# New places in the written-out order of a Mamba and FP4 feed-forward kernel on one core

## The chip, the core and the metric

The kernel runs on one core of a Trainium2 chip. Its engines are TensorE (PE in the profile, with its weight loads shown apart as PEld), VectorE (DVE), ScalarE (ACT), GpSimd (POOL) and SyncE (SP), which here issues all DMAs. The metric is the time of one launch in microseconds (us) on the device. Three runs of the kernel before gave a median of 1878.63 us (1877.05 to 1879.68).

## The reference, cut to what matters

The input x has 8 sequences of 2048 tokens with 256 features. A state-space layer and a feed-forward layer follow each other, each with a residual and a layer norm behind it. In the feed-forward layer the activations and the weights are rounded to a grid of FP4 values with one scale per 16 features.

```python
def _L0_attn_ref(x, W_in, conv_w, conv_b, W_xproj, A_log, D, W_out):
    x_proj, z = jnp.split(x @ W_in, 2, axis=-1)          # 512 channels each
    xc = conv(x_proj, 4 taps along the tokens, one filter per channel)
    x_conv = silu(xc + conv_b)
    ssm = x_conv @ W_xproj                               # 1 + 16 + 16 columns
    delta = softplus(ssm[..., 0])
    Bm, Cm = ssm[..., 1:17], ssm[..., 17:]
    h_mean = einsum('bld,bln->bdn', x_conv, delta[..., None] * Bm) / L
    y = einsum('bdn,bln->bld', h_mean, Cm) + D * x_conv
    return (y * silu(z)) @ W_out

def _L0_ffn_ref(x, w_gate, w_up, w_down):                # 704 hidden features
    h = silu(fp4_linear(x, w_gate)) * fp4_linear(x, w_up)
    return fp4_linear(h, w_down)                         # rounds x, h and the weights

x = layernorm(x + _L0_attn_ref(x, ...))
x = layernorm(x + _L0_ffn_ref(x, ...))
```

(The body of the convolution is shown in words.) h_mean is a mean over all tokens of a sequence: no token of a sequence can be finished before all of its tokens have been through the convolution.

## The kernel before

A **block** is 512 tokens of one sequence, so there are 32 blocks, four to a sequence. A **pair** is 256 tokens, half a block; its two pairs are called even and odd here (half 0 and half 1). Blocks and pairs are numbered from 0.

`begin_block` takes one block as far as the sums over tokens, channels on the partitions: `load` (SP), and for each of four groups of 128 channels `project` (PE, L601), `halo` (POOL), `fetch` (ACT), `first` (ACT, the first tap), three `tap` (DVE, L621), `silu` (ACT, L627), and later `skip` (ACT, the product with D). Then, for the whole block, `x_projection` (PE, L634), `keep_ssm` (ACT) and `by_token` (DVE). For each of four chunks of 128 tokens: `turn` (PE, L663, transposes into one PSUM buffer), `turned` (ACT, L669, copies that buffer to SBUF) and `weigh` (DVE, L674, reads the same buffer and makes delta's input). The softplus is small DVE work on 128x4 elements: `negate` (L501), `exp` (POOL, L504), `ratio` (L508 to L514), `series`, `delta`, then `delta_b` (L653, writes dB). `sums` (PE, L688) adds the block to its sequence's state, and behind a sequence's last block `mean`, `spread_mean` (L702) and `keep_mean` (L708) make hT.

`mix_block` works four blocks later (LAG): `state` (PE, L750, four PSUM buffers) and four `mix` (DVE, L761).

`finish_pair` does the rest for a pair: `zed` (PE, L794), `silu_z` (ACT), `gated` (POOL, L810, a product of two SBUF tiles), `out` (PE, L817), `residual1` (DVE, L827), layer norm 1 (`n1_stats` DVE, `n1_rstd` POOL, `n1_apply` ACT), and the rounding to FP4 (`q1_scales` L287 to L298, `q1_normalize` L310, `q1_magnify` ACT L318, `q1_add` L322, `q1_subtract` L326). Rounded values and scales then go to the other layout by DMA: `q1_turn_scales` (DVE), `q1_gather_scales` (four small DMAs to HBM), `q1_spread_scales` (one broadcast DMA back, tile q_s), `q1_turn` (a DMA transpose, tile q_gT); `q1_scale` (POOL, L391) multiplies the two. Gate and up run in three column groups (`gate`, `up` PE L840, `silu_g` ACT, `product` DVE L865). The hidden features go through the same rounding (`q2_...`, the broadcast now 704 KB, the product hqT of 128x1408), then `down` (PE, L871), `residual2` (DVE, L880), layer norm 2 and `store` (SP). The last pair goes through `finish_last` in two tiles of 128 tokens, which transposes on PE in place of DMAs.

The FP4 weights are made at the start, one rounding of gate, up and down each (`PREPARE`), between the first blocks' work.

Nothing decides the order at run time. Each piece of work is put into a list with a number, its *place*; a piece of block n has n times PERIOD added, and a finishing piece (n + LAG) times PERIOD. The list is sorted by place and the pieces are written out in this order, each instruction at the end of its engine's queue. So places say who stands behind whom in a queue; they are no times, and a unit of place is no microsecond. Buffers rotate in pools of fixed size (seven PSUM buffers of one bank in the pool `ps`), and the framework adds semaphore waits for data and for buffers.

```python
def at(base, table, name, index, f, *args):
    place = table[name]
    for i in index:
        place = place[i]
    events.append((base + place, len(events), f, args))
...
for _, _, f, args in sorted(events, key=lambda e: e[:2]):
    f(*args)
```

The places stand in four tables at the top of the file: BLOCK, PAIR (even, odd), LAST (the last pair's two tiles) and PREPARE (the weights).

Of the kernel before, what the change touches and what calls it, by code (L numbers as in the profile page):

```python
# [26 lines left out]
PERIOD = 64.0  # L27
LAG = 4
BLOCK = {
    "load": -56.2,  # L30
    "halo": (-37.7, -4.0, 38.9, 5.1),
    "project": (-2.4, 20.8, 60.7, 37.8),
    "fetch": (0.4, 26.0, 64.3, 42.7),
    "first": (15.9, 38.4, 64.5, 46.8),
    "tap": ((32.5, 53.3, 53.3), (66.1, 68.5, 74.6), (75.7, 77.2, 79.3), (67.1, 69.8, 78.4)),
    "silu": (75.3, 79.4, 88.1, 83.0),
    "skip": (190.0, 117.2, 116.7, 116.8),
    "x_projection": 97.8,
    "keep_ssm": 100.8,
    "by_token": 113.7,  # L40
    "negate": 116.9,
    "exp": 117.4,
    "ratio": 117.5,
    "series": (119.2, 119.3),
    "delta": 125.0,
    "delta_b": 126.2,
    "turn": (95.0, 93.9, 89.9, 99.5),
    "turned": (101.5, 107.0, 100.5, 115.5),
    "sums": 126.3,
    "mean": 128.4,  # L50
    "spread_mean": 133.4,
    "keep_mean": 134.7,
    "state": 77.4,
    "mix": (78.9, 77.5, 80.1, 77.9),
    "weigh": (104.6, 102.6, 97.0, 116.0),
}
# [42 lines left out]
LAST = {
    "out": (100.3, 121.0),  # L100
    "residual1": (137.9, 122.5),
    "n1_stats": (185.7, 133.0),
    "n1_rstd": (193.6, 133.1),
    "n1_apply": ((206.5,), (142.8,)),
    "q1_scales": (228.2, 169.0),
    "q1_normalize": (240.8, 172.9),
    "q1_magnify": (283.6, 192.6),
    "q1_add": (314.2, 201.7),
    "q1_subtract": (438.8, 201.9),
    "q1_scale": (452.3, 213.0),  # L110
    "turn_xq": (522.5, 215.8),
    "turned_xq": (543.6, 216.6),
    "gate_up": ((573.2, 587.2, 579.3), (326.7, 409.7, 380.2)),
    "silu_g": ((596.4, 631.2, 696.9), (403.3, 526.5, 405.8)),
    "product": ((617.5, 737.8, 704.0), (501.1, 551.9, 514.4)),
    "q2_scales": (776.2, 563.7),
    "q2_normalize": (842.6, 566.6),
    "q2_magnify": (861.1, 609.1),
    "q2_add": (963.3, 672.1),
    "q2_subtract": (993.0, 690.6),  # L120
    "q2_scale": (996.9, 705.7),
    "turn_h": ((1071.2, 1083.9), (827.7, 902.7)),
    "turned_h": ((1176.6, 1176.7), (882.6, 1019.9)),
    "down": (1214.9, 1030.2),
    "residual2": (1234.8, 1072.4),
    "n2_stats": (1280.2, 1143.6),
    "n2_rstd": (1324.6, 1241.6),
    "n2_apply": ((1395.9,), (1265.4,)),
    "store": (1488.6, 1392.9),
}  # L130
PREPARE = {
    "weights": 9.1,
    "load": (-47.3, 119.5, 195.3, 284.7, 342.4),
    "scales": (-4.4, 134.9, 205.0, 285.8, 345.2),
    "normalize": (13.6, 134.9, 221.0, 286.8, 345.3),
    "magnify": (15.9, 138.6, 222.0, 289.7, 353.8),
    "add": (83.1, 154.4, 228.8, 290.3, 358.3),
    "subtract": (96.7, 158.2, 229.8, 296.4, 360.2),
    "scale": (100.3, 170.3, 233.9, 301.2, 360.3),
    "turn": ((111.7,), (188.0, 186.6, 182.2), (252.6, 250.6, 273.0), (323.1, 329.9, 320.9, 326.8), (380.3, 387.2, 384.9, 373.7)),  # L140
}

@with_exitstack
# [973 lines left out]
```

## Time and profile before

| what | us |
|---|---|
| median of three runs (lowest to highest) | 1878.63 (1877.05 to 1879.68) |
| the profiled execution | 1877.57 |
| its span, first to last instruction | 1875.4 |
| mean clock granted to PE, share of full speed | 0.987 |

The profile is of one execution. A window's line gives, for a stretch of the span, its length, the busy time of each engine with the number of its instructions, the clock granted to PE as a share, the mean share of the DMA engines and the GB/s. A line of waits names who waited, for whom, the total in us, how often, and the longest. A line of a source line gives the number of its instructions, their least, median and greatest duration in ns, and the start of the first and the last. The clock of the first stretches of the page's slices is below one:

```profile
PEclk8899999999999999999999999999999999999997
```

Some rows of the costliest groups, for the size of the pieces (columns: busy us, mean ns of one, then idle time before):

```profile
L621 DVE SCALAR_TENSOR_TENSOR xc<-xp,cw_sb,xc 128x512 f32<-128x512 f32 x384 | 283.7, 752 | 4.9 <-ACT xc L615 3.6
...
L674 DVE SCALAR_TENSOR_TENSOR xd<-ps,w_delta_sb 128x512 bf16<-128x512 f32 x128 | 86.9, 679 | 77.0 <-ACT xct L669 76.0
```

### The profile page before, as it was taken

To read this page: it belongs to the slowest core of one execution; us is meant where nothing else is said; L and a number is where in the kernel's file an instruction comes from. 1 tells how busy PE (TensorE), PEld (TensorE's weight loads), DVE (VectorE), ACT (ScalarE), POOL (GpSimd) and SP (SyncE) were. 2 spreads that over 40 slices of the span, in tenths; PEclk is the share of its full clock that TensorE was granted. 3 is DMA by queue.
4 is the path that set the end of the run, shared out by engine and by line. 5 is a ranking of instruction groups with operands and counts; after the bars stand their busy time and mean duration, and the time that the engine had idled before them with its cause. 6 is when DMAs were issued, how large, how long until landed. Compare 5 with 4: busy or idle time off the path is not lost.

```text
span 1875.4 us, 28706 instructions
## 1 busy us (share of the span) xinstructions
PE 1815.0 (97%) x10062; PEld 1463.1 (78%) x10062; DVE 1669.2 (89%) x3087; ACT 836.1 (45%) x1426; POOL 906.5 (48%) x962
## 2 busy tenths in 40 slices
PE   5799999999999999999999999999999999999986
PEld 2468887888888888888888888788888888788874
DVE  6889999999999999899999999999999999877874
ACT  5664454444444444454444445444444444333222
POOL 1234554545454534554544554544545453465652
PEclk8899999999999999999999999999999999999997
DMA  3223344343344343434333334334334423454440
GB/s 103 67 62 85 86 100 104 82 102 92 83 104 100 83 98 90 96 93 100 93 91 98 91 85 101 103 82 102 92 80 105 103 75 84 85 114 103 100 87 23
DMA packets 248384, 170.11 MB, mean 91 GB/s; under 512 B 171952, under 2 KB 223024, under 8 KB 248240
## 3 DMA queue, kind: packets, MB, share of 16 engines
q1 hardware_dynamic: 248240, 168.28, 37.5%
q8 instruction: 80, 1.31, 0.3%
q14 instruction: 64, 0.52, 0.1%
HBM read 116.34 MB, written 20.91 MB: 73 GB/s over the span
## 4 chain that ended last, share of the span: by engine, by line
PE 72%; DVE 12%; POOL 7%; issue 5%; DMA 2%; ACT 2%; SPq 0%; POOLq 0%; DVEq 0%; ACTq 0%
PE ps L840 25%; PE ps L871 13%; PE ps L601 9%; PE ps L794 9%; PE ps L817 9%; PE ps L663 2%; DVE xc L621 2%; POOL ln_rs L552 2%; PE ps L750 1%; DVE q_amax L287 1%; PE hsum L688 1%; PE ps L634 1%; DVE q_x L310 1%; POOL ln_ve L550 1%; DMA q_s<-q_rows 1%
## 5 line engine op out<-in xcount | busy, mean ns | idle before, releaser
L871 PE MATMUL ps<-wdT,hqT 128*128 128x256 f32 x1512 | 343.6, 384 | 13.1 <-POOL hqT L391 12.9
L871 PEld LDWEIGHTS ps<-wdT,hqT 128*128 128x128 f32 x1512 | 287.5, 192 | 69.5 <-issue 17.4
L810 POOL TENSOR_TENSOR xc<-xc,sz 128x512 f32<-128x512 f32 x128 | 201.7, 1587 | 272.0 <-DVE xc L761 272.0
L840 PE MATMUL ps<-wuT,xqT 128*128 128x256 f32 (+1 forms) x1512 | 328.2, 363 | 2.1 <-DVE x L880 2.1
L840 PE MATMUL ps<-wgT,xqT 128*128 128x256 f32 (+1 forms) x1512 | 325.4, 364 | 0.3 <-POOL xqT L391 0.3
L840 PEld LDWEIGHTS ps<-wgT,xqT 128*128 128x128 f32 x1512 | 274.4, 191 | 64.3 <-issue 37.8
L840 PEld LDWEIGHTS ps<-wuT,xqT 128*128 128x128 f32 x1512 | 273.4, 190 | 43.2 <-issue 6.2
L621 DVE SCALAR_TENSOR_TENSOR xc<-xp,cw_sb,xc 128x512 f32<-128x512 f32 x384 | 283.7, 752 | 4.9 <-ACT xc L615 3.6
L550 POOL TENSOR_SCALAR ln_ve<-ln_mv 128x2 f32<-128x2 f32 (+1 forms) x130 | 75.7, 582 | 397.6 <-DVE ln_mv L545 390.9
L601 PE MATMUL ps<-xT,w_in_sb 128*128 128x512 f32 x512 | 243.4, 601 | 6.0 <-DMA xT<-in_x_t_dram 6.0
L318 ACT ACTIVATE q_w<-q_x 128x512 bf16<-128x512 f32 (+3 forms) x131 | 130.9, 999 | 256.6 <-DVE q_x L310 255.0
L794 PE MATMUL ps<-xTz,w_in_sb 128*128 128x256 f32 x1024 | 241.9, 379 | 0.0
L558 ACT ACTIVATE x<-x,ln_nb,ln_rs 128x256 f32<-128x256 f32 x256 | 142.8, 593 | 195.6 <-POOL ln_nb L555 178.3
L817 PE MATMUL ps<-w_out_sb,xc 128*128 128x256 f32 x1008 | 228.0, 379 | 0.0
L794 PEld LDWEIGHTS ps<-xTz,w_in_sb 128*128 128x128 f32 x1024 | 192.7, 190 | 25.0 <-issue 1.7
L817 PEld LDWEIGHTS ps<-w_out_sb,xc 128*128 128x128 f32 x1008 | 189.2, 190 | 24.7 <-POOL xc L810 0.2
L391 POOL TENSOR_TENSOR hqT<-q_gT,q_s 128x1408 f32<-128x1408 bf16 x63 | 181.2, 2877 | 2.4 <-DMA q_gT<-q_w 1.6
L858 ACT ACTIVATE sg<-ps 128x512 f32<-128x512 f32 (+1 forms) x189 | 104.8, 556 | 164.2 <-PE ps L840 115.8
L322 DVE SCALAR_TENSOR_TENSOR q_x<-q_w,q_x 128x512 f32<-128x512 bf16 (+3 forms) x131 | 159.3, 1216 | 4.0 <-ACT q_w L318 3.7
L601 PEld LDWEIGHTS ps<-xT,w_in_sb 128*128 128x128 f32 x512 | 95.8, 193 | 81.2 <-issue 76.1
L674 DVE SCALAR_TENSOR_TENSOR xd<-ps,w_delta_sb 128x512 bf16<-128x512 f32 x128 | 86.9, 679 | 77.0 <-ACT xct L669 76.0
L326 DVE SCALAR_TENSOR_TENSOR q_w<-q_w,q_x 128x512 bf16<-128x512 bf16 (+3 forms) x131 | 151.8, 1159 | 2.6
(115 smaller groups left out, 2487.3 us busy)
## 6 DMA issues: line engine op xcount, KB each, us to landing
q_s<-q_rows SPq DMA_DIRECT2D x63, 704.0 KB
xT<-in_x_t_dram SPq DMA_DIRECT2D x32, 512.0 KB
xTz<-in_x_t_dram SPq DMA_DIRECT2D x64, 256.0 KB
xt<-in_L_attn_x_dram SPq DMA_DIRECT2D x64, 256.0 KB
q_s<-q_rows SPq DMA_DIRECT2D x63, 256.0 KB
out_dram<-x SPq DMA_DIRECT2D x63, 256.0 KB
q_rows<-q_scT SPq DMA_DIRECT2D x252, 4.0 KB
q_rows<-q_scT SPq DMA_DIRECT2D x252, 12.0 KB
```

Of the source, the lines that this page charges most:

```text
L318: nc.scalar.activation(state["g"], state["x"], AF.Abs, scale=GRID)
L322: nc.vector.scalar_tensor_tensor(xn, w, 1.5 * GRID, xn, ALU.max, ALU.subtract)
L326: nc.vector.scalar_tensor_tensor(w, w, 1.5 * GRID, xn, ALU.max, ALU.subtract)
L391: nc.gpsimd.tensor_tensor(qT(), state["gT"], state["scT"], ALU.mult)
L558: nc.scalar.activation(r()[:, t, :], r()[:, t, :], AF.Identity, bias=v["nb"][:, t : t + 1], scale=v["rstd"][:, t : t + 1],)
L601: nc.tensor.matmul(mm, w_in_sb[:, k, c * P : (c + 1) * P], s["xT"][:, k, :], start=(k == 0), stop=(k == KM - 1),)
L621: nc.vector.scalar_tensor_tensor(acc, xp[:, k + 1 : k + 1 + T], cw_sb[:, c, k + 1 : k + 2], acc, ALU.mult, ALU.add)
L794: nc.tensor.matmul(q["mm", j][:, a, :], w_in_sb[:, k, DI + c * P : DI + (c + 1) * P], q["xT"][:, k, :], start=(k == 0), stop=(k == KM - 1),)
L810: nc.gpsimd.tensor_tensor(xc, xc, q["sz"][:, c, :], ALU.mult)
L817: nc.tensor.matmul(mm[:, t, :], s["xc"][:, c, o : o + P], w_out_sb[:, c, :], start=(c == 0), stop=(c == NC - 1),)
L840: nc.tensor.matmul(q[name, j][:, t, :n], q["xqT"][:, t * KM + k, :], wT[:, k, f0 : f0 + n], start=(k == 0), stop=(k == KM - 1),)
L871: nc.tensor.matmul(mm[:, t, :], q["hqT"][:, t * NF + j, :], wdT[t][:, j, :], start=(j == 0), stop=(j == NF),)
```

## The change

The numbers in the four tables are replaced by new ones; PERIOD, LAG, and everything below the tables stay. So every piece keeps its instructions, tiles and buffers and gets a new place in the order. The diff has a line for each name of the four tables; these are the ones that matter most for the text below.

```diff
 BLOCK = {
-    "tap": ((32.5, 53.3, 53.3), (66.1, 68.5, 74.6), (75.7, 77.2, 79.3), (67.1, 69.8, 78.4)),
-    "silu": (75.3, 79.4, 88.1, 83.0),
+    "tap": ((29.14, 47.51, 49.35), (61.51, 63.86, 69.02), (69.77, 71.43, 78.60), (70.57, 79.32, 81.67)),
+    "silu": (67.08, 83.05, 82.80, 86.47),
...
-    "x_projection": 97.8,
-    "keep_ssm": 100.8,
-    "by_token": 113.7,
-    "negate": 116.9,
-    "exp": 117.4,
-    "ratio": 117.5,
-    "series": (119.2, 119.3),
-    "delta": 125.0,
-    "delta_b": 126.2,
-    "turn": (95.0, 93.9, 89.9, 99.5),
-    "turned": (101.5, 107.0, 100.5, 115.5),
-    "sums": 126.3,
+    "x_projection": 100.62,
+    "keep_ssm": 103.94,
+    "by_token": 107.26,
+    "negate": 107.08,
+    "exp": 110.53,
+    "ratio": 114.55,
+    "series": (120.42, 120.73),
+    "delta": 123.06,
+    "delta_b": 123.24,
+    "turn": (100.18, 94.70, 93.30, 96.56),
+    "turned": (107.90, 101.13, 96.16, 120.33),
+    "sums": 128.44,
...
-    "weigh": (104.6, 102.6, 97.0, 116.0),
+    "weigh": (105.96, 103.03, 93.70, 106.97),
 }
 PAIR = {
...
-    "zed": ((24.7, 20.7), (56.5, 50.5)),
-    "silu_z": ((31.0, 31.3), (59.6, 62.5)),
-    "gated": ((81.4, 83.2), (94.3, 92.7)),
+    "zed": ((25.73, 31.85), (62.07, 64.54)),
+    "silu_z": ((31.50, 68.65), (70.65, 71.37)),
+    "gated": ((88.05, 89.53), (101.88, 108.23)),
...
-    "n1_rstd": (103.4, 130.9),
+    "n1_rstd": (104.18, 135.37),
...
-    "q1_normalize": (112.0, 139.2),
+    "q1_normalize": (114.24, 145.41),
...
-    "q1_add": (115.4, 151.8),
-    "q1_subtract": (115.9, 152.2),
+    "q1_add": (114.70, 155.11),
+    "q1_subtract": (115.32, 155.23),
...
-    "q1_spread_scales": (129.1, 153.4),
-    "q1_turn": (124.0, 156.4),
-    "q1_scale": (129.8, 158.1),
+    "q1_spread_scales": (124.94, 166.78),
+    "q1_turn": (126.58, 155.50),
+    "q1_scale": (129.41, 167.59),
...
-    "q2_scales": (156.3, 183.1),
-    "q2_normalize": (161.7, 188.6),
+    "q2_scales": (161.93, 183.91),
+    "q2_normalize": (163.51, 190.42),
...
-    "q2_add": (167.3, 197.3),
-    "q2_subtract": (168.8, 198.1),
+    "q2_add": (169.88, 203.89),
+    "q2_subtract": (175.66, 205.47),
...
-    "q2_turn": (177.9, 216.8),
-    "q2_scale": (185.5, 219.0),
-    "down": (189.0, 227.3),
-    "residual2": (205.2, 234.8),
-    "n2_stats": (213.2, 237.1),
+    "q2_turn": (181.09, 214.66),
+    "q2_scale": (182.53, 227.13),
+    "down": (192.05, 229.56),
+    "residual2": (199.43, 235.62),
+    "n2_stats": (214.13, 235.75),
...
-    "store": (221.3, 252.8),
+    "store": (223.66, 252.24),
...
 }
```

In BLOCK, `turn`, `turned` and `weigh` list the chunks 0 to 3, `silu` the channel groups; in PAIR the first number or group is the even pair's, the second the odd pair's. A piece at place 167 of one block and one at place 103 of the next stand side by side, since PERIOD is 64.

More of the change, by code (lines that the diff above doesn't have):

```diff
@@ L29 @@
 BLOCK = {
[L30 to L34, printed above, removed]
-    "tap": ((32.5, 53.3, 53.3), (66.1, 68.5, 74.6), (75.7, 77.2, 79.3), (67.1, 69.8, 78.4)),
-    "silu": (75.3, 79.4, 88.1, 83.0),
-    "skip": (190.0, 117.2, 116.7, 116.8),
-    "x_projection": 97.8,
-    "keep_ssm": 100.8,
-    "by_token": 113.7,
-    "negate": 116.9,
-    "exp": 117.4,
-    "ratio": 117.5,
@@ L44 @@
-    "series": (119.2, 119.3),
-    "delta": 125.0,
-    "delta_b": 126.2,
-    "turn": (95.0, 93.9, 89.9, 99.5),
-    "turned": (101.5, 107.0, 100.5, 115.5),
-    "sums": 126.3,
[L50 to L54, printed above, removed]
-    "weigh": (104.6, 102.6, 97.0, 116.0),
+    "load": -54.29,
+    "halo": (-6.72, -28.05, 58.44, 39.71),
+    "project": (-2.38, 26.50, 55.03, 38.59),
+    "fetch": (-2.03, 32.97, 60.17, 47.48),
@@ new lines @@
+    "first": (14.26, 40.15, 61.81, 52.44),
+    "tap": ((29.14, 47.51, 49.35), (61.51, 63.86, 69.02), (69.77, 71.43, 78.60), (70.57, 79.32, 81.67)),
+    "silu": (67.08, 83.05, 82.80, 86.47),
+    "skip": (210.79, 104.19, 208.26, 120.63),
+    "x_projection": 100.62,
[8 more added lines that the diff above has]
+    "turn": (100.18, 94.70, 93.30, 96.56),
@@ L56 @@
+    "turned": (107.90, 101.13, 96.16, 120.33),
+    "sums": 128.44,
+    "mean": 130.09,
+    "spread_mean": 130.55,
+    "keep_mean": 133.85,
+    "state": 73.25,
+    "mix": (80.53, 79.69, 79.90, 82.73),
+    "weigh": (105.96, 103.03, 93.70, 106.97),
 }
 PAIR = {
-    "load_t": (-19.1, 38.0),
-    "load_x": (90.8, 71.7),
-    "zed": ((24.7, 20.7), (56.5, 50.5)),
-    "silu_z": ((31.0, 31.3), (59.6, 62.5)),
-    "gated": ((81.4, 83.2), (94.3, 92.7)),
-    "out": (92.7, 123.2),
-    "residual1": (98.2, 127.2),
@@ L65 @@
-    "n1_stats": (101.2, 130.5),
-    "n1_rstd": (103.4, 130.9),
-    "n1_apply": ((105.3, 105.7), (133.1, 131.4)),
-    "q1_scales": (107.6, 134.8),
-    "q1_normalize": (112.0, 139.2),
-    "q1_magnify": (112.7, 141.2),
-    "q1_add": (115.4, 151.8),
-    "q1_subtract": (115.9, 152.2),
-    "q1_turn_scales": (110.5, 137.6),
-    "q1_spread_scales": (129.1, 153.4),
-    "q1_turn": (124.0, 156.4),
-    "q1_scale": (129.8, 158.1),
-    "gate": ((131.5, 133.6, 147.7), (171.1, 171.5, 167.3)),
-    "silu_g": ((134.9, 135.4, 150.8), (180.8, 177.5, 174.1)),
@@ L79 @@
-    "up": ((141.7, 144.2, 152.0), (178.5, 182.1, 167.6)),
-    "product": ((145.9, 150.8, 154.8), (181.7, 183.0, 177.0)),
-    "q2_scales": (156.3, 183.1),
-    "q2_normalize": (161.7, 188.6),
-    "q2_magnify": (164.9, 192.2),
-    "q2_add": (167.3, 197.3),
-    "q2_subtract": (168.8, 198.1),
-    "q2_turn_scales": (158.1, 185.0),
-    "q2_spread_scales": (170.8, 206.4),
-    "q2_turn": (177.9, 216.8),
-    "q2_scale": (185.5, 219.0),
-    "down": (189.0, 227.3),
-    "residual2": (205.2, 234.8),
@@ L92 @@
-    "n2_stats": (213.2, 237.1),
-    "n2_rstd": (216.2, 240.0),
-    "n2_apply": ((219.3, 220.8), (247.4, 243.4)),
-    "store": (221.3, 252.8),
-    "q1_gather_scales": (120.6, 152.1),
-    "q2_gather_scales": (163.1, 195.8),
+    "load_t": (-40.08, 58.48),
+    "load_x": (47.72, 66.29),
+    "zed": ((25.73, 31.85), (62.07, 64.54)),
+    "silu_z": ((31.50, 68.65), (70.65, 71.37)),
+    "gated": ((88.05, 89.53), (101.88, 108.23)),
+    "out": (95.70, 125.60),
+    "residual1": (99.36, 127.22),
@@ new lines @@
+    "n1_stats": (100.40, 130.53),
+    "n1_rstd": (104.18, 135.37),
+    "n1_apply": ((106.40, 106.98), (139.63, 139.26)),
+    "q1_scales": (110.08, 143.35),
+    "q1_normalize": (114.24, 145.41),
+    "q1_magnify": (114.33, 154.32),
+    "q1_add": (114.70, 155.11),
+    "q1_subtract": (115.32, 155.23),
+    "q1_turn_scales": (112.14, 152.30),
+    "q1_spread_scales": (124.94, 166.78),
+    "q1_turn": (126.58, 155.50),
+    "q1_scale": (129.41, 167.59),
+    "gate": ((139.28, 132.09, 148.78), (175.11, 173.33, 169.64)),
@@ new lines @@
+    "silu_g": ((142.54, 141.04, 149.47), (179.58, 174.55, 171.04)),
+    "up": ((151.87, 134.37, 148.79), (176.58, 174.21, 172.04)),
+    "product": ((152.91, 147.26, 150.59), (183.14, 183.10, 176.89)),
+    "q2_scales": (161.93, 183.91),
+    "q2_normalize": (163.51, 190.42),
+    "q2_magnify": (166.30, 194.41),
+    "q2_add": (169.88, 203.89),
+    "q2_subtract": (175.66, 205.47),
+    "q2_turn_scales": (163.17, 194.44),
+    "q2_spread_scales": (177.48, 211.11),
+    "q2_turn": (181.09, 214.66),
@@ L98 @@
+    "q2_scale": (182.53, 227.13),
+    "down": (192.05, 229.56),
+    "residual2": (199.43, 235.62),
+    "n2_stats": (214.13, 235.75),
+    "n2_rstd": (218.21, 245.24),
+    "n2_apply": ((222.77, 220.44), (249.66, 248.56)),
+    "store": (223.66, 252.24),
+    "q1_gather_scales": (123.69, 152.49),
+    "q2_gather_scales": (172.81, 208.53),
 }
 LAST = {
[L100 to L129, printed above, removed]
+    "out": (116.96, 124.39),
+    "residual1": (139.70, 137.78),
@@ new lines @@
+    "n1_stats": (144.79, 145.59),
+    "n1_rstd": (179.50, 151.75),
+    "n1_apply": ((184.83,), (160.37,)),
+    "q1_scales": (222.18, 167.58),
+    "q1_normalize": (249.49, 168.25),
+    "q1_magnify": (296.90, 178.65),
+    "q1_add": (348.21, 181.18),
+    "q1_subtract": (377.02, 197.36),
+    "q1_scale": (459.18, 209.24),
+    "turn_xq": (482.10, 211.41),
+    "turned_xq": (533.22, 214.19),
+    "gate_up": ((570.55, 571.33, 646.11), (305.18, 429.40, 437.31)),
+    "silu_g": ((579.04, 703.18, 708.77), (397.66, 459.08, 446.13)),
@@ new lines @@
+    "product": ((628.72, 757.14, 722.33), (397.78, 475.22, 479.00)),
+    "q2_scales": (790.70, 524.15),
+    "q2_normalize": (840.93, 536.49),
+    "q2_magnify": (870.91, 564.08),
+    "q2_add": (909.52, 581.47),
+    "q2_subtract": (949.66, 588.51),
+    "q2_scale": (1049.29, 612.74),
+    "turn_h": ((1110.93, 1050.67), (811.95, 792.95)),
+    "turned_h": ((1115.18, 1159.95), (813.51, 959.75)),
+    "down": (1207.39, 976.22),
+    "residual2": (1223.66, 1062.85),
+    "n2_stats": (1239.26, 1091.98),
@@ L130 @@
+    "n2_rstd": (1348.85, 1185.82),
+    "n2_apply": ((1418.49,), (1260.80,)),
+    "store": (1558.46, 1344.44),
 }
 PREPARE = {
[L132 to L139, printed above, removed]
@@ L140 @@
-    "turn": ((111.7,), (188.0, 186.6, 182.2), (252.6, 250.6, 273.0), (323.1, 329.9, 320.9, 326.8), (380.3, 387.2, 384.9, 373.7)),
+    "weights": 11.23,
+    "load": (-39.51, 112.43, 197.71, 273.33, 339.69),
+    "scales": (-33.38, 126.51, 210.44, 279.11, 339.70),
+    "normalize": (-17.33, 127.93, 215.67, 281.81, 340.59),
+    "magnify": (16.93, 130.87, 217.22, 286.26, 346.74),
+    "add": (53.14, 140.83, 222.52, 289.74, 354.07),
+    "subtract": (82.62, 153.80, 222.57, 290.03, 360.31),
+    "scale": (98.84, 159.37, 233.74, 296.53, 360.51),
@@ L141 @@
+    "turn": ((99.60,), (191.68, 187.04, 177.59), (272.17, 264.32, 253.93), (314.43, 315.67, 318.81, 328.50), (370.36, 382.98, 385.89, 363.76)),
 }
```

## The prediction

> **What bounds the kernel now.** I read the page's busy line first, then the windows of the stages, then the waits of TensorE (PE) and VectorE (DVE) in each stage, and last the rows of the instructions that the change moves past one another.
>
> ```profile
> PE 1815.0 (97%) x10062; PEld 1463.1 (78%) x10062; DVE 1669.2 (89%) x3087; ACT 836.1 (45%) x1426; POOL 906.5 (48%) x962
> ```
> ```profile
> 6.00:36.40 30.40, 22.51 (x88) 11.12 (x89) 18.89 (x49) 18.82 (x33) 3.87 (x10) 0.94 0.39 113
> 36.40:60.80 24.40, 16.02 (x86) 8.26 (x87) 20.24 (x44) 14.32 (x26) 5.62 (x6) 0.78 0.20 60
> 60.80:83.60 22.80, 16.77 (x80) 8.13 (x80) 20.06 (x44) 14.47 (x25) 6.00 (x6) 0.79 0.07 24
> 83.60:102.70 19.10, 18.30 (x110) 11.91 (x112) 17.38 (x44) 13.17 (x25) 3.94 (x8) 1.00 0.26 80
> ...
> 128.00:1600.00 1472.00, 1471.48 (x8297) 1193.34 (x8296) 1365.80 (x2517) 677.28 (x1151) 731.34 (x760) 1.00 0.39 93
> 1600.00:1664.00 64.00, 61.23 (x317) 52.57 (x317) 53.88 (x103) 23.73 (x40) 36.06 (x35) 0.97 0.51 101
> 1664.00:1790.00 126.00, 123.37 (x672) 109.10 (x671) 102.17 (x162) 35.74 (x57) 79.11 (x66) 1.00 0.43 99
> 1790.00:1875.40 85.40, 60.50 (x255) 50.12 (x254) 48.78 (x89) 20.46 (x39) 29.04 (x43) 0.86 0.29 56
> ```
> The columns after the stretch are its length and the busy times of PE, its weight loads, DVE, ScalarE (ACT) and GpSimd (POOL); the clock is the last but two. The first four stretches are cut at the starts of the four `sums` of blocks 0 to 3 (36.4, 60.8, 83.6, 102.7). PE is busy in 1471.48 of the 1472 us between 128 and 1600. Busy alone proves little, so its waits decide:
>
> ```profile
> PE ps L663 <- ACT xc L627: 11.4, 6, 3.7
> PE hsum L688 <- DVE dB L653: 10.2, 4, 4.4
> ...
> PE ps L601 <- DMA xT<-in_x_t_dram: 6.0, 1, 6.0
> ```
> are the waits of the first 107 us (total, times, longest). From 107 to 1600 PE waits 1.1 us in all. Behind that it waits again:
>
> ```profile
> PE hsum L688 <- DVE dB L653: 2.3, 1, 2.3
> PE ps L750 <- ACT hT L708: 0.5, 1, 0.5
> ...
> PE ps L840 <- DVE x L880: 2.1, 3, 1.2
> ...
> PE ps L871 <- POOL hqT L391: 12.1, 2, 9.2
> ```
> (the first two from 1600 to 1664, the third to 1790, the fourth to the end). So there are three stages: a head of about 107 us, where DVE is the longest queue; some 1490 us at PE's own pace; and a tail of chains.
>
> A rule speaks against this reading. The Trainium skill, Perfetto Trace Analysis, section Identifying the Most-Contended Engine, calls matmul busy time a bad measure, since matmuls are pipelined, and would have weight loads judged. These are busy in 1193 of 1472 us, 81%; by the rule up to 279 us could be open in the middle, and a better order might reach for them. The row is against it: in the chain of waits the 24 matmuls of one `down` take 5.18 us wherever they stand in the middle, so one starts each 216 ns, and no wait is left that an order could take away. I put the middle at the row's value: nothing to win.
>
> **The change part by part.** The instructions, tiles, buffers and waits for data are the same; only the numbers by which the pieces are sorted are new. The built queues have the same work: up to the fourth `sums`, DVE has 52 taps (L621), 16 `weigh` (L674) and four softplus in both. What can change is who stands behind whom.
>
> *Middle, collisions on SBUF.* In the old order `ratio` (L508, 128x4) follows `exp` at once, and so does GpSimd's hqT product:
>
> ```profile
> L508 DVE TENSOR_SCALAR sp_u<-sp_e x32: 170/2840/2882, 33.4 to 1615.5; 128x4 f32<-128x4 f32 x32
> ...
> L391 POOL TENSOR_TENSOR hqT<-q_gT,q_s 128x1408 f32<-128x1408 bf16 x63 | 181.2, 2877 | 2.4 <-DMA q_gT<-q_w 1.6
> ```
> Its least time is 170 ns, its median 2840: it stands for as long as the product beside it, 2.67 us per block. `q2_scales` (L294) has a maximum of 2168 ns beside a median of 200 for the same reason. In the new order `ratio` comes about 2.1 us after `q2_subtract` on DVE (product 0.55, tap 0.75, normalize 0.65, transpose 0.15), while the product must first wait for the DMA transpose of that result, 2.55 us at the least in the chain of waits; so `ratio` is through before. The skill's SBUF - State Buffer, section Who interferes with whom, has an exclusive lock: a DVE instruction with two SBUF inputs would stand fully beside a GpSimd product. By that rule a tap that meets L391 would cost up to 2.9 us; the trace has taps beside it at 0.88 against 0.75. By the row DVE gets 2.7 us per block back for L508 and a part of 1.6 for L294, 3 to 4 us of 55.7; by the rule more. For the time both give 0 in the middle, because PE hides it: DVE is at 1365.8 of 1472 already. If that cover were gone, it would be worth up to 28 x 2.7 = 75 us. What a collision elsewhere would cost is bounded by the same slack, 106 us over the stage.
>
> *Middle, distances.* What could be lost there: each result must still be ready when PE comes to it. Between `out` and the first gate of the odd pair, the new PE order has 40 us of work (two `down` of 5.2, four `zed` of 1.73, three `project` of 1.72, six gate and up pieces of 1.73 or 1.3, `out` 3.45, and 5 for the small ones); the chain between (residual, statistics, quantizing 1, its DMAs, product) is 17 us by its rows. From the last `up` to `down` PE has 39 us, the chain 15 to 18. So some 20 us of the lead are spare for queueing. The seven PSUM buffers are the narrower point: the even pair's second `zed` is now written at place 31.85 and read by `silu_z` at 68.65, which holds a buffer for over half a period, while the others are let go by a DVE that has gained 3 us. I take 0, range 0 to +3.
>
> *Head.* Each chunk's transposes are read from one PSUM buffer by `weigh` (DVE) and `turned` (ACT), and the trace has each waiting for the other. In the head:
>
> ```profile
> DVE xd L674 <- ACT xct L669: 11.9, 6, 3.3
> ```
> Old places: `turned0` stands before `weigh0` and `turned3` before `weigh3`, and `turned3` is late in ACT's queue; two waits in a block, 5.9, 3.2, 1.8 and 1.0 us in blocks 0 to 3. New places: only `weigh1` stands behind `turned1`. That costs at most three ACT copies of 0.58 (turned2, a fetch, turned1), 1.7 us, in blocks 0 and 1; in blocks 2 and 3 the two quantizing instructions of the weights (2 x 1.49 and 2 x 0.89) stand between and cover it. So 3.4 remain of 11.9: DVE gains 8.5. DVE is busy 76.6 of the 96.7 us to the fourth `sums`, all of it needed, and PE waits 10.2 us for its dB. But PE's 11.4 us behind `silu` stay, and ACT's queue is the next limit there. I take 5 of the 8.5, range 2 to 8.
>
> *Block 31.* Its `sums` come 2.3 us late and the state another 0.5. In front of delta_b stood the blocked `ratio` (2.67 too long) and `q2_normalize` (1.58); the new order has q1_add and q1_subtract (1.38) in its place. 2.9 earlier covers the 2.8: I take 2.8.
>
> *Tail to 1790.* Three waits for residual2 (2.1 us): old, it stood behind q2_add, q2_subtract and the other pair's q1 scales; new, in front of them, over 3 us earlier. I take 1.5 of the 2.1, as `mix` is next behind it.
>
> *Last pairs.* Here the new order adds a wait. DVE's q2_subtract of pair 62 now stands behind residual2 and n2_stats of pair 61, which need pair 61's `down`. By the timeline, q2_subtract ran from 1823.41 to 1825.04, that `down` to 1824.98, and residual2 and the statistics take 2.1 us: it would start at 1827.2, 3.8 later. Behind it wait SP's transpose, GpSimd's product and the last `down` (the 9.2 us wait). Yet the transpose took 5.95 us behind a 704 KB broadcast issued 3.3 us ahead; later it finds that done, down to 2.55. So 0.4 to 3.8 lost; I take 2.
>
> Sum: -5 - 2.8 - 1.5 + 2 = **-7.3**. The profiled execution took 1877.57 (span 1875.4 and 2.2 around it), so 1870.3; it lies 1.06 below the median of the runs, 1878.63, so 1871.3 is the forecast.
>
> **Rivals.** *The head gains little* (`silu` and ACT keep its pace: -2) and block 31's delta_b is late all the same: -2 - 1.5 + 2 = -1.5, 1877.1. For it: PE waits longer for silu than for dB. Against: it waits for dB in each of the four blocks.
> *It doesn't do what it says*: the places are no times, nothing ties GpSimd to DVE, the product may meet `ratio` after all. Then block 31's 2.8 stays: -4.5, 1874. For it: products start when DMAs land. Against: the 2.1 against 2.55 above, though thin.
> *More*: all 8.5 in the head, 2.1 in the tail, 0.4 at pair 62: -13.0, 1865.6.
> *Slower*: GpSimd's queue. The odd pair's q1 product waits for its scale broadcast, which SP now issues behind the even pair's store, and behind that product stand the even pair's n1_rstd and the odd pair's second `gated`, which PE's `out` needs. At one us of PE wait in each of 27 blocks: -7 + 27 = +20, 1899. It decides once broadcasts come so late that the spare 20 us are used up; GpSimd waits 56.3 us for q_s in 26 cases today, 3.5 at the longest, so this is far.
>
> **Chances.** Forecast 0.62, more 0.12, not as it says 0.12, head gains nothing 0.05, slower 0.09. About 0.2% (3.8 us) can be told from no change. Faster: 0.59 of the first, 0.12, half of the third: 0.77; within: 0.14; slower 0.09. The range 1866 to 1877.5 takes in 2 to 8 in the head and 0.4 to 3.8 at pair 62, and leaves out the slower case and the edge of "more".
>
> **What would show it.** L508's median near 170; DVE's waits for `turned` in the head near 3.4; the fourth `sums` at 96 to 99; PE's waits from 107 to 1600 at 1 us still, with the period of 55.7 us unchanged; no wait at block 31's `sums`; the last wait for hqT at 10 to 13 us. A PE wait that recurs in each block would make it wrong.

## The result and the profile after

| | before | after |
|---|---|---|
| median of the runs (lowest to highest) | 1879.16 us (1877.05 to 1882.02) | 1862.47 us (1861.68 to 1863.83) |
| the profiled execution, and its span | 1877.57, 1875.4 | 1862.53, 1860.7 |

The ratio is 0.9911 (95% interval 0.9894 to 0.9928): 16.7 us less, where 7.3 less were forecast and the range ended at 1866.0. The busy line of the kernel after:

```profile
PE 1806.7 (97%) x10062; PEld 1461.3 (79%) x10062; DVE 1573.0 (85%) x3087; ACT 824.5 (44%) x1426; POOL 820.8 (44%) x962
```

VectorE is 96 us less busy and GpSimd 86 us. TensorE loses 8 us of busy time with the same 10062 instructions, and its mean granted clock goes from 0.987 to 0.991; that is the first sign of what the forecast missed. The windows of the kernel after, cut at about the same events as those shown of the one before:

```profile
6.00:32.10 26.10, 21.33 (x87) 10.21 (x88) 18.85 (x49) 18.46 (x32) 3.96 (x10) 1.00 0.45 133
32.10:54.60 22.50, 14.85 (x85) 8.26 (x85) 20.11 (x44) 12.34 (x22) 4.90 (x7) 0.77 0.00 1
54.60:76.00 21.40, 13.34 (x75) 7.01 (x75) 20.40 (x44) 15.05 (x26) 4.18 (x5) 0.89 0.29 93
76.00:96.70 20.70, 20.67 (x113) 13.61 (x113) 18.98 (x45) 14.29 (x27) 3.87 (x8) 0.86 0.30 95
122.00:1594.00 1472.00, 1472.00 (x8305) 1196.14 (x8305) 1280.20 (x2523) 668.93 (x1157) 672.56 (x762) 1.00 0.39 93
1594.00:1653.60 59.60, 59.60 (x316) 51.81 (x315) 46.59 (x94) 20.97 (x37) 29.19 (x31) 1.00 0.41 98
1653.60:1779.00 125.40, 123.86 (x676) 109.83 (x676) 99.36 (x165) 38.20 (x62) 63.14 (x70) 1.00 0.43 100
1779.00:1860.70 81.70, 56.17 (x250) 46.74 (x248) 46.20 (x83) 19.11 (x36) 27.57 (x40) 0.91 0.24 56
```

In the stretch of block 31 (the sixth line) TensorE is busy throughout, at a clock of 1.00; before, the same place had 0.97 and 2.8 us of waits. TensorE's waits up to 102 us, then those from 1779 us on; between 102 and 1653 us there is none, and from there to 1779 one of 1.5 us:

```profile
PE ps L663 <- ACT xc L627: 13.6, 7, 3.8
PE ps L601 <- DMA xT<-in_x_t_dram: 6.2, 1, 6.2
PE hsum L688 <- ACT xc L627: 4.1, 1, 4.1
...
PE hsum L688 <- DVE dB L653: 1.8, 1, 1.8
```
```profile
PE ps L871 <- POOL hqT L391: 12.9, 2, 10.1
PE ps L1003 <- POOL last_h L340: 2.6, 2, 1.5
PE ps L1014 <- ACT last_qT L1009: 1.9, 3, 0.8
```

To see where the time went, I took the same events in every trace: the starts of some `state`s (L750) and of the last pairs' pieces. The state of block 28 is the first that needs block 31's sums; the expectations below call the states of blocks 27 and 28 by the blocks begun beside them, 30 and 31. All in us, the changes taken before rounding:

| stretch | forecast of the change | before | after | change |
|---|---|---|---|---|
| start to the first `state` | -5 | 106.8 | 101.2 | -5.6 |
| to the state of block 27 | 0 | 1473.0 | 1473.0 | 0.0 |
| to the state of block 28, behind block 31's sums | -2.8 | 54.4 | 49.5 | -4.9 |
| to the last state, block 31's | -1.5 | 135.2 | 133.5 | -1.8 |
| to the last tiles' first transposes, L959 (pairs 61 and 62) | +2 | 72.2 | 72.3 | +0.1 |
| to L1003 | not in the sum | 14.4 | 14.0 | -0.4 |
| to TensorE's last instruction | not in the sum | 13.2 | 11.1 | -2.1 |

These add up to -14.7, the difference of the spans. The other 2 us of the medians most likely lie in the head, which differs most between executions: with the head's queues unchanged, `state` first started at 106.8, 107.0, 108.5, 109.8 and 111.3 us in five profiled executions, and at 101.2, 102.2 and 102.9 us in three with the new ones. The profile that the forecast was summed against had the shortest head of the five.

### The profile page after: what moved, and what is told of

It reads as the page before. It is cut to its first block, busy times and chain, and to the rows that moved or that the text cites. A ratio compares the mean times of both kernels' runs of the same rounds, so it can differ in the third digit from the quotient of the medians.

```text
span 1860.7 us, 28636 instructions
## 1 busy us (share of the span) xinstructions
PE 1806.7 (97%) x10062; PEld 1461.3 (79%) x10062; DVE 1573.0 (85%) x3087; ACT 824.5 (44%) x1426; POOL 820.8 (44%) x962
## 4 chain that ended last, share of the span: by engine, by line
PE 93%; DVE 3%; POOL 1%; ACT 1%; issue 1%; DMA 1%; SPq 0%; POOLq 0%; DVEq 0%; ACTq 0%
PE ps L840 32%; PE ps L871 18%; PE ps L794 12%; PE ps L817 11%; PE ps L601 11%; PE ps L663 3%; PE ps L750 2%; PE hsum L688 2%; PE ps L634 2%; DVE xc L621 1%; POOL hqT L391 0%; DMA q_gT<-q_w 0%; DVE xd L674 0%; PE ps L702 0%; DVE q_w L326 0%
## 5 line engine op out<-in xcount | busy, mean ns | idle before, releaser
L871 PE MATMUL ps<-wdT,hqT 128*128 128x256 f32 x1512 | 342.8, 383 | 14.4 <-POOL hqT L391 14.4
L810 POOL TENSOR_TENSOR xc<-xc,sz 128x512 f32<-128x512 f32 x128 | 161.8, 1275 | 386.4 <-DVE xc L761 386.4
L794 PE MATMUL ps<-xTz,w_in_sb 128*128 128x256 f32 x1024 | 246.0, 383 | 0.0
L391 POOL TENSOR_TENSOR hqT<-q_gT,q_s 128x1408 f32<-128x1408 bf16 x63 | 191.8, 3045 | 119.3 <-DMA q_gT<-q_w 101.2
L558 ACT ACTIVATE x<-x,ln_nb,ln_rs 128x256 f32<-128x256 f32 x256 | 142.5, 596 | 123.1 <-POOL ln_nb L555 123.1
L391 POOL TENSOR_TENSOR xqT<-q_gT,q_s 128x512 f32<-128x512 bf16 x63 | 85.5, 1357 | 219.9 <-DMA q_gT<-q_w 146.8
L322 DVE SCALAR_TENSOR_TENSOR q_x<-q_w,q_x 128x512 f32<-128x512 bf16 (+3 forms) x131 | 150.4, 1148 | 15.9 <-ACT q_w L318 15.9
L865 DVE TENSOR_TENSOR h<-sg,ps 128x512 f32<-128x512 f32 (+1 forms) x189 | 119.5, 633 | 50.5 <-ACT xct L669 36.9
L326 DVE SCALAR_TENSOR_TENSOR q_w<-q_w,q_x 128x512 bf16<-128x512 bf16 (+3 forms) x131 | 150.6, 1150 | 3.3
```

Of the source, the lines that this page charges most:

```text
L322: nc.vector.scalar_tensor_tensor(xn, w, 1.5 * GRID, xn, ALU.max, ALU.subtract)
L326: nc.vector.scalar_tensor_tensor(w, w, 1.5 * GRID, xn, ALU.max, ALU.subtract)
L391: nc.gpsimd.tensor_tensor(qT(), state["gT"], state["scT"], ALU.mult)
L558: nc.scalar.activation(r()[:, t, :], r()[:, t, :], AF.Identity, bias=v["nb"][:, t : t + 1], scale=v["rstd"][:, t : t + 1],)
L794: nc.tensor.matmul(q["mm", j][:, a, :], w_in_sb[:, k, DI + c * P : DI + (c + 1) * P], q["xT"][:, k, :], start=(k == 0), stop=(k == KM - 1),)
L810: nc.gpsimd.tensor_tensor(xc, xc, q["sz"][:, c, :], ALU.mult)
```

## Experiments

Two theories stood open. For the size of the gain: TensorE's waits cost more than their length, because its clock is halved behind them. For its source: a few relations between neighbours carry all of it, not the parting of GpSimd's products and VectorE.

**b_weigh: two numbers alone.**

```diff
-    "weigh": (104.6, 102.6, 97.0, 116.0),
+    "weigh": (101.4, 102.6, 97.0, 115.4),
```

> The kernel before, with only the places of weigh changed (chunk 0 and chunk 3 now stand ahead of `turned` of the same chunk). Theory (the head gained because VectorE no longer stands behind ScalarE's copies): most of the head's gain comes with it: VectorE's waits for `turned` before 102 us fall from 11.9 to about 3 us, the first `state`, at 106.8 us in the kernel before and 101.2 in the one after, starts at 101 to 103, and the time falls by 4 to 6 us. Rival (the head's gain came from the other new places, the taps' and the weights' among them): `state` starts at 105.5 to 107 and the time falls by under 1.5 us. From 107 us on nothing changes in either.

1866.86 us (ratio 0.9938, interval 0.9923 to 0.9953): 11.6 less, far more than expected. VectorE's waits for `turned` in the head are gone wholly; what its rows (waits of VectorE to 100 us) still show for this line is

```profile
DVE xd L674 <- PE ps L663: 1.4, 4, 0.6
```

The first `state` starts at 99.1 us, and the stretch behind block 31's sums takes 51.2 instead of 54.4. `weigh` of chunk 3 no longer waits 1.19 us for its copy there, and dB is ready before TensorE comes to the sums. TensorE waits for hT instead:

```profile
1623.15 1.17 PE L750 MATMUL ps<-ct,hT 16*128 16x128 f32 x32 [1.63 <-ACT hT L708]
```

Behind this shorter wait the clock stays at 1.00, which is more than half of the 3.2 us. "From 107 us on nothing changes" was wrong by these 3.2 us; the rival is out. (The two numbers also change VectorE's own queue: chunk 0's `weigh` now stands ahead of chunk 1's, and chunk 3's ahead of q1_subtract. What this does by itself was not tested.)

**b_prod: the collision taken from the kernel before.** Only GpSimd's order changes.

```diff
-    "q2_scale": (185.5, 219.0),
+    "q2_scale": (180.9, 219.0),
```

> The kernel before, with the even pair's hqT product one step earlier in GpSimd's queue, ahead of `exp`, so that it is through when `ratio` runs. Both theories: L508's median falls from 2840 to about 170 ns and VectorE's busy time by some 70 us, and the middle keeps its period of 55.7 us. In block 31 VectorE's dB comes about 1.8 us sooner (2.67 less 0.9 by which `exp` is later), so TensorE waits about 0.5 instead of 2.3 us in front of the sums. Theory (a wait of over 2 us costs its own length and then halved-clock work): the granted clock stays at 1.00 behind that wait, and the distance from 1600 us to the last block's `state` shrinks by 3.5 to 4.5 us. Rival (only the wait counts): it shrinks by 1.8 us, clock or not.

L508's median falls from 2840 to 170 ns and the middle stays (1472.5). VectorE is only 18 us less busy, though, and not 70: L508 and L294 take 94 us less, but L326 takes 31 more, L519 23 and L322 14, so most of the gain went to other instructions. Block 31's sums wait for nothing any more. But the state right behind them now waits for hT:

```profile
1635.57 1.17 PE L750 MATMUL ps<-ct,hT 16*128 16x128 f32 x32 [2.14 <-ACT hT L708]
```

The clock falls behind that wait instead: 51.7 us for this stretch, 136.8 for the next, which had 135.2. So neither theory had it right: the wait moved to the next in line. The time is 1875.39 (ratio 0.9984, 0.9977 to 0.9990).

**b_turnh and a_last: one ScalarE copy of the last tiles, in the kernel before and undone in the one after.**

```diff
-    "turned_h": ((1176.6, 1176.7), (882.6, 1019.9)),
+    "turned_h": ((1176.6, 1176.7), (860.9, 1019.9)),
```
```diff
-    "turned_h": ((1115.18, 1159.95), (813.51, 959.75)),
+    "turned_h": ((1115.18, 1159.95), (871.50, 959.75)),
```

> The kernel before, with one ScalarE copy of the last two tiles (turned_h, tile 1, first half) ahead of the other tile's magnify instead of behind it. Theory (the last tiles' gain of 3.1 us is a wait of 2.8 us cut into short ones, after which the clock stays high): TensorE's wait of 2.81 us in front of the last `down`s is replaced by two of under 1 us, the granted clock there is 1.00 instead of 0.50, the 12 matmuls L1014 take under 3.5 us of work instead of 5.49, and the end comes 2.5 to 3.5 us sooner. Rival (the copies are not what ends that wait, the gain came from the other tile's chain): the end moves by under 1 us.

> The kernel after, with the one copy turned_h (tile 1, first half) put back behind the other tile's magnify; all other queues are the same. Theory (this one place is the last tiles' gain): one TensorE wait of 2.3 to 3 us comes back in front of the first last-tile `down`, the clock falls to 0.50 behind it, the stretch from the last tiles' first transposes L1003 to the end goes from 11.1 to 13 to 13.8 us. Rival (the rest of the new order of the last tiles carries it): under 0.8 us.

Both came as the theory had it. From L1003 to TensorE's end it takes 10.7 us in b_turnh (13.2 before) and 13.6 us in a_last (11.1 after). The times are 1876.28 (ratio 0.9992, 0.9983 to 1.0001) and 1865.61, which is 3.1 above the kernel after (their runs don't overlap). The timeline of a_last at this place (start, length, what, count, and in brackets the wait):

```profile
1844.40 0.87 PE L1003 MATMUL ps<-ident,last_h 128*128 128x128 f32 x6 [1.14 <-POOL last_h L340]
1848.18 5.49 PE L1014 MATMUL ps<-wdT,last_qT 128*128 128x256 f32 x12 [2.91 <-ACT last_qT L1009]
1853.47 1.12 PE L1003 MATMUL ps<-ident,last_h 128*128 128x128 f32 x6
1855.15 2.86 PE L1014 MATMUL ps<-wdT,last_qT 128*128 128x256 f32 x12 [0.57 <-ACT last_qT L1009]
```

The same 12 matmuls take 5.49 us behind a wait of 2.91 and 2.86 behind one of 0.57. The window of the former in the kernel before, where it was the same:

```profile
1859.70:1865.00 5.30, 5.26 (x12) 4.10 (x13) 1.44 (x2) 0.37 (x1) 1.38 (x1) 0.50 0.01 3
```

A clock of 0.50. And the kernel after, with the copy in front, has the wait in pieces and no halved clock behind them:

```profile
1844.93 1.56 PE L1014 MATMUL ps<-wdT,last_qT 128*128 128x256 f32 x6 [0.57 <-ACT last_qT L1009]
1847.27 1.56 PE L1014 MATMUL ps<-wdT,last_qT 128*128 128x256 f32 x6 [0.77 <-ACT last_qT L1009]
```

Its waits from L1003 to the end add up to 3.4 us (0.57, 0.77, 1.45, 0.57), those of the kernel before to 3.0 (2.81, 0.16). So it does not wait less; the gain is clock.

**b_fill and b_fill2: is it the clock?** Both keep every wait for data and put matmuls into it whose results nobody reads.

```diff
+    def fill(k):
+        mm = bank()
+        for _ in range(k):
+            nc.tensor.matmul(mm[:, :FW], ident, w_in_sb[:, 0, :FW], start=True, stop=True)
```

> The kernel before, with 20 added TensorE matmuls whose results nobody reads (128x256, 216 ns each): 9 in front of block 31's `sums`, 11 in front of the first last-tile `down`, inside waits of 2.27 and 2.81 us. No wait for data is shortened and no other instruction moves. Theory (behind a wait of over 2 us the clock is halved for some 3 to 4 us, and that costs work): the clock stays at 1.00 in both places; from 1600 us to the last block's `state` it takes 1.6 to 2.2 us less, the 12 matmuls L1014 take 2.9 instead of 5.5 us, and the time falls by 4 to 5 us in all. Rival (the low clock in the record costs nothing, or falls for another reason): nothing gained at either place, or 0.2 us lost.

> The kernel before, again with added matmuls that nobody reads in front of block 31's `sums` and of the first last-tile `down`, but 4 and 5 of them (432 ns each, 1.7 and 2.2 us) in waits of 2.3 and 2.8 us, so that they don't outlast the waits as the first try's did. Theory (halved clock behind a wait costs 2 us in block 31 and 3 us at the last tiles): the clock stays at 1.00 at both, the distance between the last two `state`s shrinks from 54.4 to 52.2 to 52.8 us, and the stretch from the last tiles' first transposes L1003 to the end shrinks from 19.3 to 16 to 17 us; the time falls by 4 to 5 us. Rival (the first try's fillers only broke even because low clock costs nothing): no gain.

In b_fill each fill matmul ran as two of 216 ns, so the fillers outlasted the waits by some 2 us; the times, 1877.42 (0.9995, 0.9986 to 1.0003) and 1879.75 (1.0000, 0.9991 to 1.0010), tell nothing. The places do. At the last tiles, b_fill:

```profile
1858.64 4.91 PE L1067 MATMUL ps<-w_in_sb,ident 128*128 128x256 f32 x22
1863.39 2.75 PE L1014 MATMUL ps<-wdT,last_qT 128*128 128x256 f32 x12
```

2.75 us for what took 5.49, with nothing changed but that TensorE was kept busy. In b_fill2, with fillers of the right length, L1003 to the end takes 10.7 us instead of 13.2. So the halved clock is a cost, and it is on the path here. In block 31 the expectation failed: the clock stays up behind the sums, but the distance stays 54.4 in both, and in b_fill2 the state then waits 2.14 us for hT, as in b_prod. With the clock up, TensorE only comes sooner to a result that isn't there.

**b_five: what makes hT late.** The chain behind block 31's sums in the kernel before, from its timeline:

```profile
1628.30 1.50 POOL L550 TENSOR_SCALAR ln_ve<-ln_mv 128x2 f32<-128x2 f32 x1 [6.26 <-DVE ln_mv L545]
1629.88 2.07 POOL L552 TENSOR_TENSOR ln_rs<-ln_ve,m_half 128x2 f32<-128x2 f32 x1
1632.57 1.09 ACT L558 ACTIVATE x<-x,ln_nb,ln_rs 128x256 f32<-128x256 f32 x2 [3.95 <-POOL ln_nb L555]
1633.56 0.56 ACT L708 COPY hT<-ps 128x512 f32<-128x512 f32 x1
...
1634.18 1.17 PE L750 MATMUL ps<-ct,hT 16*128 16x128 f32 x32 [0.50 <-ACT hT L708]
```

keep_mean (L708) needs only L702, which was through by 1631.95. But in ScalarE's queue it stands behind two n1_apply (L558), and these wait for GpSimd's n1_rstd, whose two first operations take 1.50 and 2.07 us beside VectorE's q2_add and q2_subtract (0.22 and 0.71 where VectorE is elsewhere). The test puts n1_apply behind keep_mean, with the numbers of b_weigh and b_turnh:

```diff
-    "n1_apply": ((105.3, 105.7), (133.1, 131.4)),
+    "n1_apply": ((105.3, 105.7), (134.75, 134.72)),
```

> The kernel before, with five numbers changed: `weigh` of chunks 0 and 3 ahead of `turned`, both n1_apply of the odd pair behind keep_mean on ScalarE, and one turned_h of the last tiles ahead of the other tile's magnify. Theory (what sets block 31's state is keep_mean, queued on ScalarE behind two n1_apply which wait for n1_rstd on GpSimd; dB was only the first of two waits): the distance between the states of blocks 30 and 31 is 49.5 to 49.9 us, against 54.4 before and 51.2 with the two `weigh` places alone, no wait for hT is left there, and the last tiles end 2.2 to 2.8 us sooner; the time is 1861.5 to 1864.5, level with the kernel after, whose other 180 numbers then bring nothing. Rival (hT is late for another reason): the distance stays at 51.2 and the time at 1864.5 to 1866.

```profile
1616.77 1.50 POOL L550 TENSOR_SCALAR ln_ve<-ln_mv 128x2 f32<-128x2 f32 x1 [5.31 <-DVE ln_mv L545]
1618.35 2.07 POOL L552 TENSOR_TENSOR ln_rs<-ln_ve,m_half 128x2 f32<-128x2 f32 x1
1619.26 0.59 ACT L708 COPY hT<-ps 128x512 f32<-128x512 f32 x1 [2.16 <-PE ps L702]
1620.88 1.17 PE L750 MATMUL ps<-ct,hT 16*128 16x128 f32 x32
```

GpSimd is as slow as before, but hT no longer stands behind it, and the state comes without a wait, 49.5 us behind the last, as in the kernel after. The time is 1863.60 us (ratio 0.9919, 0.9904 to 0.9934; runs from 1862.0 to 1864.1): level with the kernel after, from five numbers. Its busy line and its row for `ratio` are

```profile
PE 1808.2 (97%) x10062; PEld 1460.2 (79%) x10062; DVE 1679.2 (90%) x3087; ACT 835.3 (45%) x1426; POOL 907.6 (49%) x962
```
```profile
L508 DVE TENSOR_SCALAR sp_u<-sp_e x32: 170/2848/2887, 29.6 to 1603.7; 128x4 f32<-128x4 f32 x32
```

The collisions are still there, and VectorE is busy for 106 us more than in the kernel after. In time they cost nothing: the middle takes 1472.8 us here and 1473.0 there. (That the rest of the new order brings nothing would be too much: it is 2.1 us shorter in the tail than b_five, and b_five has a head shorter by 2.7.)

**a_ratio: the collision put back into the kernel after.**

```diff
-    "ratio": 114.55,
+    "ratio": 119.12,
```

> The kernel after, with `ratio` moved behind the first of the odd pair's products, so that it meets GpSimd's hqT product again. Theory (the collision is hidden everywhere in the new order, in block 31 too, where dB is done 5.3 us ahead of its sums): L508's median rises from 164 to 2000 to 2900 ns, VectorE's busy time by 50 to 80 us, and the time stays within 1 us of the kernel after. Rival (the collision's removal is what brought part of the gain): the time rises by 2 us or more, by 0.1 us per block or in block 31.

L508's median is 2250 ns, VectorE's busy time 1637.7 (65 more), the time 1863.44: 1.0 above the kernel after, with runs that overlap (1861.89 to 1864.33). Of the 1.9 by which its span is longer, 1.7 lie in the head, where executions differ by that much; from the first `state` on, the stretches are those of the kernel after but for 0.2 us. No sign of the rival.

**a_weigh: the one `weigh` that still stands behind `turned`.**

```diff
-    "weigh": (105.96, 103.03, 93.70, 106.97),
+    "weigh": (105.96, 100.90, 93.70, 106.97),
```

> The kernel after, with one number changed: `weigh` of chunk 1 gets a place ahead of `turned` of the same chunk (100.90 for 103.03). VectorE's queue keeps its order; only who of the two readers of the buffer goes first changes. Theory (each microsecond that VectorE stands behind ScalarE's copies in the head is on the path): VectorE's waits for `turned` in the head fall from 3.6 us to under 0.5, the first `state` comes at 98 to 100 us instead of 101.2, the time falls by 1.5 to 3 us. Rival (the rest of the head is already paced by `silu`): under 0.7 us.

The waits for `turned` are gone, and `state` starts at 98.1 us in the profiled execution (100.6 in a_two, which has the same change). But that was its shortest; the median is 1861.69 (1859.51 to 1863.92), 0.8 below the kernel after. Between the two expectations, and not told apart.

**a_fill, a_two and a_two_fill: what is left to win.** a_fill puts fillers into three waits of the kernel after; a_two is a_weigh with the even pair's q2_subtract ahead of residual2; a_two_fill is a_two with the fillers.

```diff
-    "q2_subtract": (175.66, 205.47),
+    "q2_subtract": (171.50, 205.47),
```

> The kernel after, with added matmuls that nobody reads in three of its waits: 8 in front of block 2's `sums` (wait 4.1 us), 5 in front of pair 61's `down` (2.8 us) and 21 in front of pair 62's `down` (10.1 us), 432 ns each. Theory: the clock stays at 1.00 behind all three; the first `state` comes 2 to 2.5 us sooner, the two `down`s take 5.2 to 5.4 us instead of 7.06 and 7.00, and the end comes 4.5 to 5.5 us sooner, about 1857.5. Rival (the low clock is a mere by-product and the queues behind it set the end): under 1 us.

> The kernel after, with `weigh` of chunk 1 ahead of `turned` and the even pair's q2_subtract ahead of the odd pair's residual2 (171.50 for 175.66). Theory (pair 62's subtraction waits for pair 61's `down` without need): q2_subtract of pair 62 starts right behind its q2_add, 3.4 us sooner; its DMA transpose, which lands behind the broadcast, about 1 us sooner; so the distance from the last block's mix state to pair 62's `down` falls from 65.5 to 64 to 64.8 us, and the time by 1 us from that, 1 to 3 us with the head's. Rival (the transpose lands with the broadcast, whenever it is issued): 65.3 to 65.7, and only the head's part.

> The kernel a_two with added matmuls that nobody reads in three waits: 8 in front of block 2's `sums`, 6 and 20 in front of the `down`s of pairs 61 and 62. Theory (the earlier filled run lost its gain only to a DMA that happened to land later): both `down`s take 5.2 to 5.5 us instead of 7.1, and the last block's mix state to the first last-tile transposes L959 takes 69.5 to 71 us instead of 72.3; the head gains about 1 us; the time is 2 to 3.5 us below a_two. Rival (the fillers themselves delay the transfers, or the chain behind the transfers sets the end): L959 stays at 72 to 72.6 and the time within 1 us of a_two.

a_fill took 1862.90 us, no gain: the last `down` took 5.45 us instead of 7.00, but the two `down`s started 1.7 and 1.8 us later, since GpSimd waited 1.7 us for the transfers of pair 61's hqT, where it hadn't. Whether the fillers have to do with that is open. Nor did the head gain: the clock stayed up behind the filler there, and the first `state` still came at 102.1 us. a_two took 1863.59: its rival holds, and the price is higher than it said. The transpose was issued 2.0 us behind the broadcast instead of 6.7, and pair 62's `down` started at 66.7 us behind the last state, not at 65.5; 1.1 us more went in the middle (1474.1). In the 14 traces pair 62's hqT product starts 8.6 to 10.5 us behind the issue of the broadcast: 8.6 to 9.5 where the transpose was issued 3.3 us behind it, 9.7 to 10.5 where it was 6.0 to 6.8, and 10.4 in a_two, with 2.0. a_two_fill took 1860.19 (1857.67 to 1860.63), ratio 0.9899 (0.9882 to 0.9916): 2.3 below the kernel after with no overlap of the runs, 3.4 below a_two. It is the shortest of all, though not as expected: L959 came at 72.6, and only the first of the two `down`s kept its clock. Of the 4.5 us between the spans of the two profiled executions, 3.3 lie in the head, where executions of one order differ by as much, so how much of the gain is the fillers' is not shown.

```profile
1803.63 5.45 PE L871 MATMUL ps<-wdT,hqT 128*128 128x256 f32 x24 [1.25 <-POOL hqT L391]
...
1819.98 7.10 PE L871 MATMUL ps<-wdT,hqT 128*128 128x256 f32 x24 [2.27 <-POOL hqT L391]
```

Behind the first filler 1.25 us of wait remained, behind the second 2.27.

## Why the prediction was right in direction and wrong in size

*The signs that it named came, and the time was still outside.* L508's median is 164 ns; VectorE waits 3.6 us for `turned` in the head (forecast 3.4); the fourth sums are at 96.7 (96 to 99); TensorE waits for nothing between 102 and 1653 us; the period is the same; the last wait for hqT is 10.1 (10 to 13). These signs told of the mechanisms that were in the sum. None told of what was left out of it.

*Middle, 0: right,* and by its reason. 1473.0 us in both, with VectorE 86 us less busy in it. a_ratio and b_five show the cover from both sides. The weight-load rule would have left 279 us open there; no order run here took any of it. The rule of the exclusive lock and the row agreed on the time, as said. But the taps of 0.88 us that the prediction set against the rule stood beside the short product xqT and the `gated` behind it; none met hqT's. In the kernel after, 13 taps do, like this one:

```profile
359.92 0.75 DVE L621 SCALAR_TENSOR_TENSOR xc<-xp,cw_sb,xc 128x512 f32<-128x512 f32 x1
360.02 3.39 POOL L391 TENSOR_TENSOR hqT<-q_gT,q_s 128x1408 f32<-128x1408 bf16 x1
```

The tap began first and took its usual time; the product took 3.39 us instead of 2.88. So the trace does not speak against the rule: here it is the product that stands.

*Head, -5: right in size* (-5.6 in the two profiles, and -6.6 between the means of the executions with each order), 8.3 of 11.9 us of waits being taken away. The cap was real and a little looser than forecast: TensorE's waits for dB fell from 10.2 to 1.8 us, but those for `silu` (L627) grew from 11.4 to 17.7. b_weigh takes away all 11.9 and gets 7.7.

*Block 31, -2.8: the step that failed* (-4.9). "2.9 earlier covers the 2.8: I take 2.8" prices two waits by their length. TensorE's clock in the stretch behind them stood in the trace of before (here a window of it):

```profile
1627.00:1630.40 3.40, 3.40 (x14) 2.07 (x7) 3.26 (x7) 0.80 (x2) 2.02 (x2) 0.50 0.57 150
```

The trace's record of the clock has it at 0.50 for 3.41 us there: 1.7 us of lost work. With 2.3 and 0.5 of waits, and 0.3 of one for hqT in the same stretch, that is 4.8 of the 4.9 that the change brought. The Trainium skill, TensorE: Matmul & The Clock Gate, section Terms, gives this price (time throttled, times one less the share of the clock), and the sum left it out. The step also looked at dB alone. Where only dB comes earlier, the wait goes to hT: in b_weigh 1.63 us of it are left, the clock stays up, and 3.2 us are gained; in b_prod 2.14 are left, the clock falls, and of 2.7 us gained 1.6 are lost again in the next stretch. The other 1.7 us needed keep_mean ahead of n1_apply on ScalarE (b_five), which the new order had and the prediction did not look at.

*Tail, -1.5: right* (-1.8); the waits for residual2 in it are gone.

*Last pairs, +2: too high* (+0.1). The transpose is issued 3.4 us later behind the broadcast, about as late as said, but the product behind it comes only 1.0 us later: pair 62's `down` starts 0.6 us later, and runs 0.6 us shorter, as the clock is back sooner.

*The last tiles: missing.* The table LAST was among the new places and got no term. One copy in it is worth 2.1 to 2.6 us in the profiled executions, all of it clock.

So of the 7.4 us by which the spans' difference passed the sum, 2.1 are block 31 (1.7 of it clock), 2.5 what follows L959, 1.9 pair 62, 0.6 the head and 0.3 the tail. The range was too narrow mainly because it bounded the costs of the terms, and not the terms that weren't there: the clock behind the waits, and the last tiles.

## What to carry to other kernels

Price a wait of TensorE with the clock behind it: read the granted clock in the windows that follow, and where it is 0.50 and TensorE has work, add half their length. Splitting such a wait, or filling it with idle matmuls, can save this part, if the next result is there. Before a removed wait is booked, ask what the next result stands behind in its own queue: here hT stood behind two instructions that it didn't need. And when a whole table of an order is replaced, give each stage a term, even if it is "unknown, between these two".

## What the runs showed of the hardware

*How short a wait halves the clock.* The skill's page on the clock gate (TensorE: Matmul & The Clock Gate, section What's actually happening) speaks of an idle window of about 3.4 us. Here shorter waits were enough: waits of 2.14, 2.27, 2.81 and 2.91 us were followed by a clock of 0.50; waits of 1.25, 1.63 and 1.84 weren't, and neither was one of 2.63 in a_two. So between 2 and 3 us it can go either way. Two waits close together can do it too: 1.1 and 1.45 us, 0.3 us apart, in the head, where the kernel after and its variants all have them; the clock fell with them in a_last, a_ratio, a_fill and a_two, and not in the other three.

*What it costs.* The record of the clock changes in steps: in all 14 traces every low stretch, but for the last of each record, lasts 3.41, 6.83, 10.24 or 13.65 us, so a short wait costs about 1.7 us or more if it costs any and TensorE has work in the whole stretch. Two runs show it behind the wait for hT: 3.41 us low in b_prod and 1.6 us lost in the next stretch, 6.83 and 3.4 in b_fill2. The same wait can cost more or less: the last tiles' wait of 2.81 us has 6.83 us of low clock behind it in the kernel before and 3.41 in b_prod, where nothing was changed at this place; the 12 matmuls took 5.49 and 4.30 us.

*GpSimd stands too.* The collision of the prediction works in the other direction: 128x2 operations of n1_rstd took 1.50 and 2.07 us beside VectorE's 128x1408 q2_add and q2_subtract, against 0.22 and 0.71. In each case looked at here the one that began later stood: `ratio` began 0.06 us behind the product (1615.46 and 1615.40 us, block 31 before), n1_rstd's two operations 0.17 and 0.12 behind q2_add and q2_subtract, and hqT's product 0.1 behind the tap.

*A transpose lands late behind a broadcast.* Issued 2.0 to 6.8 us behind a 704 KB broadcast, it let the product start 8.6 to 10.5 us behind the broadcast's issue. Issuing it later by 3.4 us cost about 1 us; issuing it sooner, at 2.0 us, gained nothing in the one run that did so. Why is open.
